# Decoder experts: where four final norms stand in VectorE's queue

## The chip, the cores and the metric

The kernel is one launch on one core of a Trainium2 chip. The metric is the device time of the launch in microseconds; a time is the median of several runs. Engines are called as in the profile: PE is TensorE (PEld its weight loads), DVE is VectorE, ACT is ScalarE, POOL is GpSimd, SP is SyncE, which here only issues DMAs.

## The reference

Two decoder layers work on 16 batches of 128 tokens by 512 features. Each layer has three blocks, each with a residual sum and a layer norm behind it:

```python
def _layernorm(x, axis=-1, eps=1e-05):
    m = jnp.mean(x, axis=axis, keepdims=True)
    v = jnp.var(x, axis=axis, keepdims=True)
    return (x - m) / jnp.sqrt(v + eps)
...
x = _layernorm(x + _L0_attn_ref(x, ...))    # state space scan
x = _layernorm(x + _L0_xattn_ref(x, ctx, ...))
x = _layernorm(x + _L0_ffn_ref(x, ...))
x = _layernorm(x + _L1_attn_ref(x, ...))
x = _layernorm(x + _L1_xattn_ref(x, ctx, ...))
x = _layernorm(x + _L1_ffn_ref(x, ...))     # 8 groups of experts
return x
```

The change touches only what follows the last block, so that block matters. It routes each token to 8 of 64 experts in 8 groups of 8 and sums over the groups that the token reaches:

```python
scores = softmax(x @ gate_w.T)
topk_w, topk_idx = top_k(scores, 8)
w_e = zeros((N, 64)).at[arange(N)[:, None], topk_idx].add(topk_w)
flat = w_e[:, inv_map]                      # N x 8 groups x 8
scalar = flat.sum(-1)
soft = softmax(where(flat == 0, NEG_INF, flat), axis=-1)
xg = x[:, None, :] + einsum('ngi,ghi->ngh', soft, mask_up_w)
a = silu(einsum('ngh,gih->ngi', xg, gate_proj_w)) * einsum('ngh,gih->ngi', xg, up_proj_w)
y = einsum('ng,ngh->nh', scalar, einsum('ngi,ghi->ngh', a, down_proj_w))
```

## The kernel before

Five stages follow one another: `stage_ssm`, `stage_xattn`, `stage_ffn`, `stage_attention`, `stage_moe`. The residual stream stays in SBUF as 16 tiles `k.x[b]`, one for each batch.

The expert stage, `stage_moe`, works on two halves of 8 batches. The router (`Moe.route`) has scattered a copy of each token's row into a bucket in DRAM for each group that the token reaches. Each half's buckets hold up to 768 rows, six tiles of 128. A *unit* is one such tile of one group: units 0 to 47 are the first half's 8 groups, units 48 to 89 seven groups of the second half, and the last group of the second half is done for all tokens of its 8 batches, in order, without a bucket (units 90 to 97).

One software-pipelined loop, `for t in range(-5, len(units) + 4)`, runs over the units. A step `t` does the following parts, each for another unit, named by their distance:

- `fetch` (unit t+5): SP loads the tile `row` from its bucket, six buffers.
- `places` (t+3) and `masks` (t+2): PE transposes part of the row (`pts`, L1507) and multiplies by the mask weights (`pm`, L1513); DVE adds the row: `xg` (L1515).
- `turn_in` (t+1): four PE transposes `ptx` of `xg` (L375, in `transpose4`), copied by ACT into `xgT` (L1521).
- `gate_up` (t): 16 PE matmuls into `pg` and `pu` (L1529), one PSUM buffer each; ACT takes `act` from `pg` (L1532), DVE multiplies it with `pu` (L1533).
- `turn_act` (t-1): PE transposes `pta` (L1539), ACT copies `aT` (L1541).
- `down` and `store` (t-2): six PE matmuls `y` (L1546); DVE copies `y` into `yo` (L1556), and ACT issues the store `results<-yo` (L1557).

The weights of a group, `gu` and `dn` (`Moe.load`), are loaded by SP into two buffers, one group ahead.

Once a unit's result is stored, `Moe.combine` runs as a generator, one `yield` a step. POOL gathers the group's results for one batch into `got` (L1565), three steps later POOL adds them to `k.x[b]` (L1572), and four steps later, in the last group of the first half and for every second batch, `self.finish(b - 1)` writes the final norm of two batches. So the norms of batches 0/1, 2/3, 4/5 and 6/7 are written as the generators of these pairs end. `finish` calls `layernorm` (statistics L68, aggregate L69, scaling L72) and with it `rsqrt` (three Newton steps of small operations, L53 to L58), all on DVE, and then issues two `out` transfers on SP (L1582). The norms of the second half are written by `store`, at the end of the kernel.

The order in which the program writes instructions is not the order in which an engine runs them. A scheduler orders each engine's instructions by when it takes their operands to be ready; each engine then works through its queue strictly in that order, waiting at each instruction for its semaphores. `tc.keep_in_program_order(ins)` binds an instruction behind what has been written before it for the same engine. Before the change only some PE transposes and matmuls elsewhere use it, by the class `Side`. In the compiled queue of before, the norms of the first half stand among the DVE instructions of steps 45 to 50. As the program writes them, they come at the ends of steps 53, 55 and 57 (two pairs in the last).

Of the kernel before, what the change touches and what calls it, by code (L numbers as in the profile page):

```python
# [13 lines left out]
I32 = mybir.dt.int32  # L14
U8 = mybir.dt.uint8
AF = mybir.ActivationFunctionType
ALU = mybir.AluOpType
# [25 lines left out]
        self.n += 1  # L43


def rsqrt(k, v, n, eps, scale=1.0):


    nc = k.nc
    a = k.small.tile([P, n], F32, tag=f"rs_a{n}", name="rs_a")  # L50
    y = k.small.tile([P, n], F32, tag=f"rs_y{n}", name="rs_y")
    t = k.small.tile([P, n], F32, tag=f"rs_t{n}", name="rs_t")
    nc.vector.tensor_scalar(a, v, scale, eps, ALU.mult, ALU.add)  # L53
    nc.vector.tensor_scalar(y.bitcast(I32), a.bitcast(I32), -0.5, 1597463007.0, ALU.mult, ALU.add)
    for _ in range(3):
        nc.vector.tensor_tensor(t, y, y, ALU.mult)
        nc.vector.scalar_tensor_tensor(t, t, -0.5, a, ALU.mult, ALU.mult)
        nc.vector.scalar_tensor_tensor(y, t, 1.5, y, ALU.add, ALU.mult)  # L58
    return y


def layernorm(k, ins, outs, eps=1e-5):

    nc, n = k.nc, len(ins)
    mv = k.small.tile([P, n, 2], F32, tag=f"ln_mv{n}", name="ln_mv")
    for i, r in enumerate(ins):
        st = k.small.tile([P, nc.vector.BN_STATS_DIM], F32, tag="ln_st", name="ln_st")
        nc.vector.bn_stats(st, r)  # L68
        nc.vector.bn_aggr(mv[:, i, :], st)  # L69
    rstd = rsqrt(k, mv[:, :, 1], n, eps)  # L70
    for i, (r, o) in enumerate(zip(ins, outs)):
        nc.vector.tensor_scalar(o, r, mv[:, i, 0:1], rstd[:, i : i + 1], ALU.subtract, ALU.mult)  # L72


def stage_ssm(k):
# [9 lines left out]
    with ExitStack() as ctx:  # L85
# [96 lines left out]
        def output(p, ys):  # L182

            mv = k.small.tile([P, BQ, 2], F32, tag="s1_mv", name="s1_mv")
            xs = k.x[p * BQ : (p + 1) * BQ]
            for i, x in enumerate(xs):
                po = bank("BA"[i], [P, D], "po")
                for c in range(KC):
                    nc.tensor.matmul(po, ys[c // 2][:, c % 2, i * P : (i + 1) * P], outw[:, c], start=c == 0, stop=False)
                nc.tensor.matmul(po, ones[32:33, 0:P], rows[32:33], start=False, stop=True)  # L190
                nc.vector.tensor_tensor(x, po, x, ALU.add)
                st = k.small.tile([P, nc.vector.BN_STATS_DIM], F32, tag="ln_st", name="ln_st")
                nc.vector.bn_stats(st, x)
                nc.vector.bn_aggr(mv[:, i, :], st)
                yield
            rstd = rsqrt(k, mv[:, :, 1], BQ, 1e-5)
            shift = k.small.tile([P, BQ], F32, tag="s1_sh", name="s1_sh")
            nc.vector.scalar_tensor_tensor(shift, mv[:, :, 0], -1.0, rstd, ALU.mult, ALU.mult)
            for i, x in enumerate(xs):
                nc.scalar.activation(x, x, AF.Identity, scale=rstd[:, i : i + 1], bias=shift[:, i : i + 1])  # L200
            yield
# [202 lines left out]
def stage_xattn(k):  # L404
# [9 lines left out]
    with ExitStack() as ctx:  # L414
# [54 lines left out]
        def project(b):  # L469
# [44 lines left out]
            yield  # L514
            nc.scalar.copy(st.v[:, 0], ps)
            rk = rsqrt(k, ss[:, 0:8], 8, EPS, 1.0 / HD)
            for s, kr in enumerate(krs):
                nc.gpsimd.tensor_tensor(kr, kr, rk[:, 4 * s : 4 * s + 4].unsqueeze(2).to_broadcast([P, 4, HD]), ALU.mult)
# [71 lines left out]
        def outputs(st, g):  # L590

            yield
            ao = pao.tile([P, J * P], F32, tag="ao", name="ao")
            for s in range(2):
                nc.tensor.matmul(
                    ao, st.v[:, s, g * HD : (g + 1) * HD], st.pTs[g][:, s].rearrange("p j t -> p (j t)"), start=s == 0, stop=s == 1
                )
            yield
            aT = wk.tile([P, J, P], F32, tag="aT", name="aT", bufs=3)
            nc.vector.tensor_copy(aT.rearrange("p h t -> p (h t)"), ao)  # L600
            yield
            if g == 0:
                st.po = pao.tile([P, D], F32, tag="po", name="po")
            for j in range(J):
                h = g * J + j
                nc.tensor.matmul(st.po, aT[:, j], k.wo[h // 8][:, h % 8], start=h == 0, stop=h == G * J - 1)  # L606
            yield
            if g == G - 1:
                nc.vector.tensor_tensor(k.x[st.b], st.po, k.x[st.b], ALU.add)
                yield  # L610
                if st.b % 2:
                    xs = k.x[st.b - 1 : st.b + 1]
                    layernorm(k, xs, xs)
                    yield
# [92 lines left out]
def stage_ffn(k):  # L707
# [4 lines left out]
    with ExitStack() as ctx:  # L712
# [8 lines left out]
        def prepare(st):  # L721

            xn = [wk.tile([P, D], F32, tag="xn", name="xn") for _ in st.xs]
            layernorm(k, st.xs, xn, 1e-8)
            yield
            qs, st.step = quantize(k, xn)
            yield
            st.qT = []
            for q in qs:
                st.qT.append(transpose_q(k, po_, q))  # L730
                yield

        def finish(st):
            layernorm(k, st.xs, st.xs)
            yield
# [9 lines left out]
        for n, sn in enumerate(states):  # L745
            nxt = prepare(states[n + 1]) if n + 1 < len(states) else iter(())
            for i, x in enumerate(sn.xs):
                st = sn.step[:, i : i + 1]
                po = po_.tile([P, D], F32, tag="po", name="po")
                for h in range(HB):  # L750
# [24 lines left out]
                    if n and h >= 2:  # L775
                        next(ahead, None)
                nc.vector.tensor_tensor(x, po, x, ALU.add)
            late = finish(sn)
        for _ in late:
            pass  # L780
# [517 lines left out]
class Moe:  # L1298
# [260 lines left out]
    def combine(self, h, g, n):  # L1559

        k, nc, b = self.k, self.nc, h * (NB // 2) + n
        got = self.wk.tile([P, D], F32, tag="got", name="got", bufs=10)

        end = 1 + min(P * (n + 1), self.CAP)
        nc.gpsimd.indirect_dma_start(  # L1565
            out=got[:, :], out_offset=None, in_=k.results[h][g][0:end, :],
            in_offset=bass.IndirectOffsetOnAxis(ap=self.gidx[:, b, g : g + 1], axis=0),
        )
        yield
        yield  # L1570
        yield
        nc.gpsimd.tensor_tensor(k.x[b], got, k.x[b], ALU.add)  # L1572
        for _ in range(4):
            yield
        if g == self.NG - 1 and n % 2:
            self.finish(b - 1)

    def finish(self, b):
        xs = self.k.x[b : b + 2]
        layernorm(self.k, xs, xs)  # L1580
        for i, x in enumerate(xs):
            self.nc.sync.dma_start(self.k.args["out"][b + i], x)  # L1582

# [209 lines left out]
```

## Time and profile before

| | |
|---|---|
| median of 3 runs | 3377.56 us (3376.58 to 3380.5) |
| profiled execution | 3382.4 us, of which the span is 3380.6 us |
| granted PE clock, mean over the span | 0.965 |
| busy PE / DVE / ACT / POOL | 3153.0 / 1876.7 / 1379.5 / 1389.5 us |
| L1529, `pg` and `pu`, 784 matmuls each | 301.7 and 299.6 us |
| L1546, `y`, 588 matmuls | 268.3 us |
| L1572, POOL's sums, 120 | 152.2 us, 1274 ns each |
| L68, norm statistics, 96 | 65.4 us, 687 ns each |
| L1582, `out` transfers, 16 | issued from 2924.5 to 3374.7 us |

Busy time is the sum of the instructions' durations on an engine; the engines work beside each other, so the sums do not add up to the span. In the rows of a timeline the first number is the start in us from the span's begin, the second the length of one or of several merged instructions, then engine, line, operation, output and inputs. A bracket at the end holds the idle time of that engine just before, and what ended it. The names leave out buffer numbers: `x` is any of the 16 tiles.

### The profile page before, as it was taken

How to read it: one execution, taken by the hardware profiler on the slowest of the kernel's cores; microseconds unless marked ns; L12 is line 12 of the kernel's file. 1: busy time of each engine (PE TensorE's matmuls, PEld its weight loads, DVE VectorE, ACT ScalarE, POOL GpSimd, SP SyncE). 2: the span in 40 equal slices, each digit the busy share in tenths (PEclk: the TensorE clock that was granted, in tenths of full speed). 3: DMA queues.
4: the chain of work that ended last, by engine and by line, in shares of the span. 5: the costliest groups of instructions: out<-in, count | busy, mean ns of one | idle time of the engine just before them, and what ended most of it. 6: DMA issues, size and time to landing. Idle time of an engine off the chain costs nothing. (4 is left out here: it accounts for less than half of the span.)

```text
span 3380.6 us, 38522 instructions
## 1 busy us (share of the span) xinstructions
PE 3153.0 (93%) x12894; PEld 1813.6 (54%) x12944; DVE 1876.7 (56%) x4202; ACT 1379.5 (41%) x3299; POOL 1389.5 (41%) x1198
## 2 busy tenths in 40 slices
PE   6888999899999999999799989998989999989998
PEld 3444444355555555555466555665655566556665
DVE  5877888456556556455576669765643232222223
ACT  4655655133333233234333379865643232112221
POOL 6967887133323333332000066325624454233331
PEclk8999999899999999999899989999999999999999
DMA  6887332200000000002200010013335665445441
GB/s 230 261 259 223 98 88 69 68 7 4 7 4 4 7 4 4 7 1 94 91 1 1 17 47 1 11 57 148 137 133 175 201 233 189 163 156 172 163 158 65
DMA packets 161553, 317.28 MB, mean 94 GB/s; under 512 B 19113, under 2 KB 82089, under 8 KB 158276
## 3 DMA queue, kind: packets, MB, share of 16 engines
q1 hardware_dynamic: 123012, 215.83, 20.8%
q0 software_dynamic: 19328, 64.56, 5.5%
q10 hardware_dynamic: 19008, 34.35, 2.7%
q8 instruction: 105, 1.72, 0.2%
q14 instruction: 100, 0.82, 0.1%
HBM read 238.80 MB, written 129.04 MB: 109 GB/s over the span
## 5 line engine op out<-in xcount | busy, mean ns | idle before, releaser
L245 POOL TENSOR_TENSOR dBx<-dtx,BC 128x1024 f32<-128x1024 f32 x128 | 301.2, 2373 | 44.8 <-DVE h L258 35.1
L1529 PE MATMUL pg<-gu,xgT 128*128 128x352 f32 x784 | 301.7, 467 | 0.0
L1529 PE MATMUL pu<-gu,xgT 128*128 128x352 f32 x784 | 299.6, 464 | 0.0
L1546 PE MATMUL y<-dn,aT 128*128 128x512 f32 x588 | 268.3, 592 | 0.0
L1533 DVE SCALAR_TENSOR_TENSOR act<-pu,row,act 128x352 f32<-128x352 f32 x98 | 57.1, 583 | 376.3 <-PE pu L1529 317.9
L575 POOL TENSOR_TENSOR pr<-pr,sm 128x512 f32<-128x512 f32 x128 | 134.7, 1053 | 289.6 <-DVE sm L574 244.2
L236 ACT ACTIVATE h<-dt,negA 128x254 f32<-128x254 f32 x512 | 239.8, 474 | 14.9 <-DVE dt L178 2.1
L1572 POOL TENSOR_TENSOR x<-got,x 128x512 f32<-128x512 f32 x120 | 152.2, 1274 | 226.4 <-DMA got<-results,gidx 225.2
L606 PE MATMUL po<-w,aT 128*128 128x512 f32 x512 | 232.2, 597 | 1.1 <-DVE aT L600 1.1
L483 PE MATMUL pq<-w,xT 128*128 128x512 f32 x512 | 228.9, 594 | 0.0
L1565 POOL DMA_INDIRECT got<-results,gidx x120 | 116.2, 968 | 268.9 <-DMA results<-yo 216.1
L460 POOL TENSOR_TENSOR m<-m,m 128x512 f32<-128x512 f32 x96 | 121.6, 1267 | 247.0 <-DVE m L455 247.0
L258 DVE TENSOR_TENSOR_SCAN h<-h,dBx 128x1024 f32<-128x1024 f32 x80 | 183.0, 2294 | 71.0 <-ACT h L236 48.7
L568 ACT ACTIVATE pr<-sc,mx,sf 128x256 f32<-128x256 f32 x256 | 142.8, 562 | 187.0 <-DVE mx L561 176.1
L267 PE MATMUL py<-hC,ident 128*128 128x512 f32 x320 | 164.6, 643 | 49.1 <-ACT y L272 49.1
L1529 PEld LDWEIGHTS pu<-gu,xgT 128*128 128x128 f32 x784 | 151.2, 193 | 85.1 <-issue 4.2
L1529 PEld LDWEIGHTS pg<-gu,xgT 128*128 128x128 f32 x784 | 144.1, 194 | 64.7 <-issue 3.0
L1532 ACT ACTIVATE act<-pg 128x352 f32<-128x352 f32 x98 | 45.5, 464 | 318.6 <-PE pg L1529 248.9
L1546 PEld LDWEIGHTS y<-dn,aT 128*128 128x128 f32 x588 | 104.1, 190 | 100.8 <-issue 94.2
L1521 ACT COPY xgT<-ptx 128x512 f32<-128x512 f32 x98 | 57.5, 587 | 233.9 <-PE ptx L375 209.6
L483 PEld LDWEIGHTS pq<-w,xT 128*128 128x128 f32 x512 | 93.5, 190 | 102.0 <-issue 99.0
L606 PEld LDWEIGHTS po<-w,aT 128*128 128x128 f32 x512 | 95.4, 191 | 96.9 <-issue 92.9
(363 smaller groups left out, 6808.3 us busy)
## 6 DMA issues: line engine op xcount, KB each, us to landing
bucket<-zeros SPq DMA_DIRECT2D x96, 388.0 KB
row<-bucket SPq DMA_DIRECT2D x90, 388.0 KB
BC<-bcd SPq DMA_DIRECT2D x128, 256.0 KB
results<-yo ACTq DMA_DIRECT2D x90, 256.0 KB
gu<-in_moe_guT SPq DMA_DIRECT2D x16, 1408.0 KB
cT<-in_ctxT SPq DMA_DIRECT2D x32, 256.0 KB
dn<-in_moe_downT SPq DMA_DIRECT2D x16, 512.0 KB
rows<-r_row SPq DMA_DIRECT2D x16, 388.0 KB
```

What stands on the lines that cost most here:

```text
L236: nc.scalar.activation(h[:, c, :, 1:], st.dt[:, c].rearrange("p (b t) -> p b t", b=BQ)[:, :, 1:], AF.Exp, scale=negA[:, c, n : n + 1])
L245: nc.gpsimd.tensor_tensor(dBx, st.dtx, BC[:, 0].unsqueeze(1).to_broadcast([P, KC, TQ]), ALU.mult)
L258: nc.vector.tensor_tensor_scan(hf, hf, df, 0.0, ALU.mult, ALU.add)
L267: nc.tensor.matmul(st.py[c], k.ident, st.hC[n][:, 2 * c : 2 * c + 2], start=n == 0, stop=n == NS - 1)
L460: nc.gpsimd.tensor_tensor(m1, m1, m2, ALU.add)
L483: nc.tensor.matmul(ps, src[:, c], w[c], start=c == 0, stop=c == KC - 1)
L568: nc.scalar.activation(pr[:, j], st.sc[g, i][:, j], AF.Exp, scale=st.sf[:, h : h + 1], bias=st.mx[g, i][:, j : j + 1], accum_out=sm[:, j : ...
L575: nc.gpsimd.tensor_tensor(pr, pr, sm.unsqueeze(2).to_broadcast([P, 2, 2 * P]), ALU.mult)
L606: nc.tensor.matmul(st.po, aT[:, j], k.wo[h // 8][:, h % 8], start=h == 0, stop=h == G * J - 1)
L1529: nc.tensor.matmul(ps, u.xT[:, c], gu[:, c, lo : lo + I], start=c == 0, stop=c == KC - 1)
L1546: self.nc.tensor.matmul(u.y, u.aT[:, c], u.w[1][:, c], start=c == 0, stop=c == 2)
L1572: nc.gpsimd.tensor_tensor(k.x[b], got, k.x[b], ALU.add)
```

## The change

`rsqrt` and `layernorm` take a function `keep` and apply it to each DVE instruction that they write. By default it does nothing. The first half's call of `finish` passes `tc.keep_in_program_order`, and it is written two steps later than before, so at the ends of steps 55, 57 and 59. The second half's norms pass no `keep`. What is computed stays the same.

```diff
-def rsqrt(k, v, n, eps, scale=1.0):
+def rsqrt(k, v, n, eps, scale=1.0, keep=lambda ins: ins):
...
-    nc.vector.tensor_scalar(a, v, scale, eps, ALU.mult, ALU.add)
+    keep(nc.vector.tensor_scalar(a, v, scale, eps, ALU.mult, ALU.add))
...
-        nc.vector.tensor_tensor(t, y, y, ALU.mult)
+        keep(nc.vector.tensor_tensor(t, y, y, ALU.mult))
...
-def layernorm(k, ins, outs, eps=1e-5):
+def layernorm(k, ins, outs, eps=1e-5, keep=lambda ins: ins):
...
-        nc.vector.bn_stats(st, r)
-        nc.vector.bn_aggr(mv[:, i, :], st)
-    rstd = rsqrt(k, mv[:, :, 1], n, eps)
+        keep(nc.vector.bn_stats(st, r))
+        keep(nc.vector.bn_aggr(mv[:, i, :], st))
+    rstd = rsqrt(k, mv[:, :, 1], n, eps, keep=keep)
...
-        nc.vector.tensor_scalar(o, r, mv[:, i, 0:1], rstd[:, i : i + 1], ALU.subtract, ALU.mult)
+        keep(nc.vector.tensor_scalar(o, r, mv[:, i, 0:1], rstd[:, i : i + 1], ALU.subtract, ALU.mult))
...
         if g == self.NG - 1 and n % 2:
-            self.finish(b - 1)
-
-    def finish(self, b):
+            for _ in range(2):
+                yield
+            self.finish(b - 1, self.k.tc.keep_in_program_order)
+
+    def finish(self, b, keep=lambda ins: ins):
         xs = self.k.x[b : b + 2]
-        layernorm(self.k, xs, xs)
+        layernorm(self.k, xs, xs, keep=keep)
         for i, x in enumerate(xs):
             self.nc.sync.dma_start(self.k.args["out"][b + i], x)
```

More of the change, by code (lines that the diff above doesn't have):

```diff
@@ L52, in rsqrt @@
     t = k.small.tile([P, n], F32, tag=f"rs_t{n}", name="rs_t")
-    nc.vector.tensor_scalar(a, v, scale, eps, ALU.mult, ALU.add)
-    nc.vector.tensor_scalar(y.bitcast(I32), a.bitcast(I32), -0.5, 1597463007.0, ALU.mult, ALU.add)
+    keep(nc.vector.tensor_scalar(a, v, scale, eps, ALU.mult, ALU.add))
+    keep(nc.vector.tensor_scalar(y.bitcast(I32), a.bitcast(I32), -0.5, 1597463007.0, ALU.mult, ALU.add))
     for _ in range(3):
-        nc.vector.tensor_tensor(t, y, y, ALU.mult)
-        nc.vector.scalar_tensor_tensor(t, t, -0.5, a, ALU.mult, ALU.mult)
-        nc.vector.scalar_tensor_tensor(y, t, 1.5, y, ALU.add, ALU.mult)
+        keep(nc.vector.tensor_tensor(t, y, y, ALU.mult))
+        keep(nc.vector.scalar_tensor_tensor(t, t, -0.5, a, ALU.mult, ALU.mult))
+        keep(nc.vector.scalar_tensor_tensor(y, t, 1.5, y, ALU.add, ALU.mult))
     return y
-def layernorm(k, ins, outs, eps=1e-5):
+def layernorm(k, ins, outs, eps=1e-5, keep=lambda ins: ins):
     nc, n = k.nc, len(ins)
@@ L1575, in combine @@
         if g == self.NG - 1 and n % 2:
-            self.finish(b - 1)
-    def finish(self, b):
+            for _ in range(2):
+                yield
+            self.finish(b - 1, k.tc.keep_in_program_order)
+    def finish(self, b, keep=lambda ins: ins):
         xs = self.k.x[b : b + 2]
-        layernorm(self.k, xs, xs)
+        layernorm(self.k, xs, xs, keep=keep)
         for i, x in enumerate(xs):
```

## The prediction

> **What bounds the kernel now.** I read the page's busy shares first: PE is busy 3153.0 of 3380.6 us (93%), so a gain must come from PE's few idle places. Then I followed the chain of work that ended last. In the expert stage it is PE at one constant beat, except between 2889 and 2976 us, where it leaves PE and goes round by DVE, two DMAs and POOL. The waits of 2880 to 2990 us name the two links:
>
> ```profile
> DVE ln_st L68 <- POOL x L1572: 38.1, 7, 8.4
> PE ptx L375 <- DVE xg L1515: 14.4, 5, 7.3
> ```
>
> Columns: us in total, times, the longest. DVE stood 38.1 us in front of seven statistics of a final norm (L68) whose batch POOL had not yet summed; PE stood 14.4 us in front of five transposes (L375) that need `xg`, queued on DVE behind them. The windows cut this at PE's `y` matmuls: six steps before the disturbance, the five disturbed steps together, six steps after, then the two worst alone (length, then busy time of PE, PEld, DVE, ACT and POOL, granted clock, DMA share, GB/s):
>
> ```profile
> 2872.21:2922.74 50.53, 50.53 (x188) 30.75 (x187) 12.94 (x29) 9.48 (x23) 16.84 (x15) 1.00 0.48 155
> 2922.74:2983.68 60.94, 46.54 (x157) 27.33 (x156) 23.56 (x75) 8.66 (x22) 16.75 (x15) 0.92 0.49 163
> 2983.68:3034.20 50.52, 50.52 (x188) 30.74 (x187) 11.34 (x20) 10.19 (x25) 17.86 (x16) 1.00 0.52 165
> ...
> 2932.06:2945.76 13.70, 10.30 (x33) 6.01 (x32) 4.59 (x15) 1.59 (x4) 3.50 (x3) 0.88 0.27 86
> ...
> 2965.80:2983.52 17.72, 10.40 (x34) 6.19 (x32) 9.68 (x37) 2.14 (x6) 6.65 (x6) 0.81 0.40 134
> ```
>
> A normal step is 50.53 / 6 = 8.42 us with PE full. The middle row holds five steps, so it is 60.94 - 5 x 8.42 = 18.84 us too long. PE's timeline shows the idle part at each transpose:
>
> ```profile
> 2926.19 0.63 PE L375 MATMUL ptx<-ident,xg 128*128 128x128 f32 x4 [0.87 <-DVE xg L1515]
> 2938.20 0.78 PE L375 MATMUL ptx<-ident,xg 128*128 128x128 f32 x4 [3.40 <-DVE xg L1515]
> 2949.38 0.63 PE L375 MATMUL ptx<-ident,xg 128*128 128x128 f32 x4 [0.87 <-DVE xg L1515]
> 2959.93 0.63 PE L375 MATMUL ptx<-ident,xg 128*128 128x128 f32 x4 [1.94 <-DVE xg L1515]
> 2975.86 1.09 PE L375 MATMUL ptx<-ident,xg 128*128 128x128 f32 x4 [7.32 <-DVE xg L1515]
> ```
>
> That is 14.40 us idle. The other 4.4 us are matmuls run slower right after a stall: 13.70 - 8.42 - 3.40 = 1.9 us and 17.72 - 8.42 - 7.32 = 2.0 us in the two steps whose clock is 0.88 and 0.81, 0.2 us in each of the others.
>
> **The change, part by part.** I number a step by the unit whose gate and up matmuls it holds. In DVE's compiled queue of before, the four norms of batches 0 to 7 lie in steps 45 to 50, each first statistic in front of `yo`. In the changed queue they lie behind `yo` of steps 55, 57 and 59, the fourth running over into step 60. Nothing is added: DVE still does 8 statistics, 8 aggregates, 44 small operations and 8 scalings. No instruction on PE, ACT or POOL changes place; on SP only the eight `out` transfers move.
>
> *Removed:* the seven waits on POOL. They made `yo` late, with it ACT's store, ACT's `act` queued behind that store, DVE's `act` and `xg`, and so PE's transpose. Gain: 18.84 us, all of it, since both neighbours of the stretch run with PE full at clock 1.00, and every chain piece after 2976 us up to the last units is PE. What is late next in those steps is PE itself.
>
> *The waits at the new place.* POOL's last sums for batches 0 to 7 end at 2911 to 2969 us. Step 55's `yo` starts at 3011.56 us, less 18.84 = 2992.7 us; the last pair's norm comes four steps later, at about 3032 us. Each sum is at least 57 us early. Cost 0, cover 57 us.
>
> *The DVE time at the new place.* The stretch that it must fit into, from DVE's and PE's timelines (start, length, idle before in brackets):
>
> ```profile
> 2986.30 0.69 DVE L1556 COPY yo<-y 128x512 f32<-128x512 f32 x1 [1.99 <-PE y L1546]
> 2991.53 0.58 DVE L1533 SCALAR_TENSOR_TENSOR act<-pu,row,act 128x352 f32<-128x352 f32 x1 [4.54 <-PE pu L1529]
> 2992.03 0.69 DVE L1515 TENSOR_TENSOR xg<-pm,row 128x512 f32<-128x512 f32 x1
> 2994.52 0.60 PE L375 MATMUL ptx<-ident,xg 128*128 128x128 f32 x4
> ```
>
> A norm with no wait in it is the last one of the kernel:
>
> ```profile
> 3370.57 0.69 DVE L68 BATCH_NORM_STATS2 ln_st<-x 128x6 f32<-128x512 f32 x1
> 3371.29 0.18 DVE L69 BATCH_NORM_AGGREGATE ln_mv<-ln_st 128x2 f32<-128x6 f32 x1
> 3371.51 0.17 DVE L53 TENSOR_SCALAR rs_a<-ln_mv 128x2 f32<-128x2 f32 x1
> 3373.68 1.00 DVE L72 TENSOR_SCALAR x<-x,ln_mv,rs_y 128x512 f32<-128x512 f32 x2
> ```
>
> Statistics to aggregate 0.72, aggregate to the second statistics 0.10, again 0.72, aggregate to the inverse root 0.22, its eleven operations 2.17, both scalings 0.9: 4.83 us. `yo` lets the next instruction start after 0.60 us, so `act` comes 0.60 + 4.83 - (2991.53 - 2986.30) = 0.20 us late. `xg` ends at 2992.72 and in the disturbed steps a transpose follows its end by 0.15 us (2938.05 to 2938.20), so `xg` may be 2994.52 - 2992.72 - 0.15 = 1.65 us late for nothing. Steps 55 and 57 cost PE 0. In step 60 a whole norm and one statistic (0.60) lie in front of `act`, and an aggregate and a statistic (0.7) between `act` and `xg`: `xg` is 0.20 + 0.60 + 0.70 = 1.5 us late, just inside 1.65. Cost 0, but this cover is nearly used up. `yo` of step 60 is about 0.9 us late; nothing on ACT's queue behind its store is due for 3 us.
>
> *POOL beside the norms.* In before the norms mostly began when POOL had just finished; now they start on a schedule and can meet POOL at work. One pair of rows shows a meeting:
>
> ```profile
> 2965.26 3.72 POOL L1572 TENSOR_TENSOR x<-got,x 128x512 f32<-128x512 f32 x3 [1.80 <-DMA got<-results,gidx]
> ...
> 2968.40 0.60 DVE L53 TENSOR_SCALAR rs_a<-ln_mv 128x2 f32<-128x2 f32 x1
> ```
>
> The small operation normally takes 0.17 us; here it ended (2969.00) with POOL's third sum (2968.98), while a statistic at 2967.79 ran its usual 0.69 us beside the same sum. The Trainium skill, "SBUF — State Buffer", section "Who interferes with whom", speaks against the change here: VectorE's second port pair is shared with GpSimd under an exclusive lock, and an instruction with two SBUF inputs or in a two-port mode is blocked for GpSimd's whole instruction. Nearly every small operation of the norm qualifies. By that rule at its worst, all POOL time of a step, 17.86 / 6 = 3.0 us, is added to a norm: against 1.65 - 0.20 = 1.45 us of cover 1.5 us in each of steps 55 and 57, against 0.15 us 2.8 us in step 60, together 5.8 us. By the rows, POOL in before does this in the stretches of the same steps:
>
> ```profile
> 3029.70 1.27 POOL L1572 TENSOR_TENSOR x<-got,x 128x512 f32<-128x512 f32 x1 [3.02 <-DMA got<-results,gidx]
> ```
>
> It meets the norm of step 57 (3029.0 to 3033.8 on that clock), mostly its statistics, and holds the first small operation by some 0.2 us; nothing of POOL falls on steps 55 or 59; in step 60 a gather (3051.43) meets a statistic, and a sum (3055.47) the tail behind `yo`. I take 0 and keep 5.8 us as the bad end. A gain from here is excluded: PE has no idle time left there.
>
> *SP's queue.* The eight transfers move from between the row fetches of units 52 to 57 to behind the weights of group 10 (`dn`, step 55), between the fetches of units 61 to 67, in pairs, each just after its norm. In before, the first pair held `gu` of group 9 to 2925.43 us where the beat of 50.53 us (2871.57 before) puts it at 2922.10. In after, a row fetch is free only when `act` of six units earlier is done, and that is queued behind the same norm, so an `out` in front of it adds its issue, about 0.4 us a transfer. A row is first read three steps (25 us) later, and `gu` of group 11, issued in step 59, in step 66. Cost 0.
>
> Sum: 18.84 gained, 0 paid. The profiled execution took 3382.4 us with a span of 3380.6; its like after the change is 3361.8 us of span, 3363.6 in all. That execution stands 4.84 us above the median of the timed runs, 3377.56. From the median: 3377.56 - 18.84 = 3358.7 us, 0.56% less.
>
> **The rivals.** *A part only (7 to 14 us gained).* The stall depends on how late gathers land, and the timed runs could hold less of it: were the whole 4.84 us between profile and median missing stall, the gain there would be 14.0 us, 3363.6 us. A half-paid gain also comes if the port lock strikes at its worst: 3358.7 + 5.8 = 3364.5. Against both: the beat is the same to 0.01 us on both sides of the stretch, and POOL's timeline leaves the new places nearly free. With some new wait of rows or weights in steps 45 to 50 I would expect about 3368 us; against it, no such wait shows in the six steps before or after.
>
> *Nothing moves (within 0.2%).* The stall is covered by another of the same size at the same place. Against: DMA share is 0.5 there, as in its full-speed neighbours; it would need 12 us or more of new stall.
>
> *Slower.* The pinned norm still finds POOL behind, and now nothing can be put in front of it: `act`, `xg`, ACT's store and SP's row fetches wait with it. It decides once POOL's sums come more than 57 us (their lead) and 1.45 us (DVE's cover) later than in this trace. To be slower by over 6.8 us the four norms must cost 18.84 + 6.8 = 25.6 us, 6.4 us each and so a lag of about 65 us: 3358.7 + 25.6 = 3384.3 us. POOL is busy 18 of every 50 us and drains each group within the next, so I give this little.
>
> **How the numbers follow.** 0.2% is 6.8 us, about what a measurement of this kernel can tell from no change. Full gain 0.87; a part 0.07; nothing 0.03; slower 0.03. So faster 0.94, same 0.03, slower 0.03. Range: down to 3354.8 (the runs of before spread over 3.9 us, so one such spread below the forecast), up to 3364.7, which takes in both ends of the partial case (3363.6 and 3364.5).
>
> **What would show it.** Right: no wait of DVE's L68 on POOL behind step 44; every `y` to `y` distance 8.42 us through steps 45 to 66; clock 1.00; the `out` issues behind `dn` of group 10; span near 3361.8. Wrong: a transpose L375 idle on `xg` in steps 56 to 61 (the norms don't fit), rs operations of over 0.5 us (port), a PE wait on `row` or `gu` (SP), or L68 waiting on POOL at the new place.

## The result, and the profile after

The changed kernel took 3364.69 us (median of 6 runs, 3356.05 to 3368.03), the kernel before on the same chip 3377.31 us (6 runs, 3376.58 to 3382.89): a ratio of 0.9951 with a 95% interval of 0.9941 to 0.9961. It is faster, by 12.6 us, where the forecast had 18.84; the time lies 0.01 us inside the upper end of the stated range, 3364.7. The profiled execution took 3364.07 us with a span of 3362.3 us, where the forecast had 3363.6 and 3361.8.

In the stretch that the change touches, the trace agrees with the forecast. (That the whole spans agree to 0.5 us is partly luck: these are single executions, and the work ahead of the expert loop alone differs by up to 9 us between the traces below.) The chain of work that ended last, by engine, from the page of after:

```profile
PE 21%; DVE 0%; issue 0%; DMA 0%; POOL 0%; ACT 0%; POOLq 0%; DVEq 0%; ACTq 0%
```

Before it was PE 19%, DMA 2%, DVE and POOL 1% each; the detour over gathers, sums and statistics is gone from it. Three stretches of six steps each from where the stall began, as windows of after (length, busy time of PE, PEld, DVE, ACT and POOL, granted clock, DMA share, GB/s):

```profile
2922.58:2973.11 50.53, 50.53 (x188) 30.74 (x187) 11.34 (x18) 10.20 (x24) 18.09 (x17) 1.00 0.49 164
2973.11:3023.63 50.52, 50.52 (x188) 30.75 (x187) 20.60 (x52) 10.20 (x24) 17.87 (x16) 1.00 0.57 187
3023.63:3074.17 50.54, 50.54 (x188) 30.76 (x187) 20.42 (x52) 10.20 (x24) 17.76 (x16) 1.00 0.56 185
```

PE is full and its clock 1.00 throughout. DVE's work has moved: 11.34 us in the first row, where before it did the norms, and 20.60 and 20.42 in the next two, where it does them now. Over 2880 to 3100 us the waits of after have no row of L68 on POOL and none of a PE transpose on `xg`; the first rows are the ordinary ones of the beat:

```profile
DVE act L1533 <- PE pu L1529: 105.5, 24, 4.6
ACT act L1532 <- PE pg L1529: 82.2, 24, 3.5
```

The tightest place is the fourth norm, from DVE's timeline of after:

```profile
3023.74 0.58 DVE L1533 SCALAR_TENSOR_TENSOR act<-pu,row,act 128x352 f32<-128x352 f32 x1 [4.56 <-PE pu L1529]
3024.24 0.68 DVE L1515 TENSOR_TENSOR xg<-pm,row 128x512 f32<-128x512 f32 x1
...
3032.94 0.57 DVE L1533 SCALAR_TENSOR_TENSOR act<-pu,row,act 128x352 f32<-128x352 f32 x1
3033.43 0.17 DVE L69 BATCH_NORM_AGGREGATE ln_mv<-ln_st 128x2 f32<-128x6 f32 x1
3033.51 0.66 DVE L68 BATCH_NORM_STATS2 ln_st<-x 128x6 f32<-128x512 f32 x1
3034.09 0.68 DVE L1515 TENSOR_TENSOR xg<-pm,row 128x512 f32<-128x512 f32 x1
```

The upper `xg` belongs to step 59, the lower to step 60. One beat later than 3024.24 would be 3032.66; it starts at 3034.09, 1.43 us late (1.5 forecast, 1.65 allowed), and PE's transpose comes on time at 3035.13. SP issues the `out` pairs at 2998.32, 3015.97, 3031.99 and 3039.07 us, and no PE instruction waits for a row or a weight.

### The profile page after: what moved, and what is told of

Its sections match the earlier page's. It is cut to its first block, busy times and chain, and to the rows that moved or that the text cites. A ratio compares the mean times of both kernels' runs of the same rounds, so it can differ in the third digit from the quotient of the medians.

```text
span 3362.3 us, 38572 instructions
## 1 busy us (share of the span) xinstructions
PE 3155.7 (94%) x12944; PEld 1814.9 (54%) x12944; DVE 1877.8 (56%) x4202; ACT 1380.7 (41%) x3299; POOL 1390.6 (41%) x1198
## 5 line engine op out<-in xcount | busy, mean ns | idle before, releaser
L1556 DVE COPY yo<-y 128x512 f32<-128x512 f32 x90 | 62.2, 692 | 158.0 <-PE y L1546 142.4
```

## The experiments

My theory: the seven waits are all that the change takes away, they cost their full 18 to 19 us in every run, and the norms cost nothing where they stand now. The rivals: timed runs hold a shorter stall than the trace of before; or the norms cost PE some 6 us at the new place, through the port that DVE shares with POOL. Either would explain 12.6 us instead of 18.84.

To compare the traces I took the starts of PE's `y` matmuls, one for each step, and subtracted 8.42 us a step. "Too long" below means that.

**The two halves of the change.** `e1_pin_only` keeps the norms in order but leaves out the two steps; `e2_late_only` has the two steps but leaves the order to the scheduler.

```diff
# e1_pin_only, against the change
-            for _ in range(2):
-                yield
             self.finish(b - 1, k.tc.keep_in_program_order)
# e2_late_only, against the change
-            self.finish(b - 1, k.tc.keep_in_program_order)
+            self.finish(b - 1)
```

> One part alone: the norms are kept in their written place, but written at the old steps, so they stand behind yo of steps 53, 55 and 57 instead of 55, 57 and 59. Theory (the place behind finished sums is what counts, and two steps more or less do not): POOL's sums are still over 40 us early, no wait of L68 on POOL, the same time as the change within 0.1%, so about 3364 us by the timed runs. Rival (the two steps are needed because the sums come late in some runs): L68 waits on POOL again and part of the 12 us is lost, 3367 us or more.

> The other part alone: written two steps later, but not kept there, so the scheduler places the norms itself. DVE's and SP's compiled queues come out as in the kernel before, so the run is also a second trace of the old order. Theory: nothing is gained, 3377 us within 0.2%, and the stretch of steps 47 to 51 is again 18 to 19 us longer than five steps of 8.42 us; the 6 us that the timed runs lack against the forecast then lie in the spread of the other stages. Rival (the trace of before was an execution with a long stall, and most have less): the stretch is only 12 to 15 us too long.

`e1_pin_only` took 3365.07 us (ratio to before 0.9946, 0.9933 to 0.9959), `e2_late_only` 3383.24 us (1.0003, 0.9995 to 1.0011); the runs of before beside them had a median of 3383.18 us (19 runs). So keeping the order is nearly the whole change; two steps later without it is nothing, since the scheduler puts the norms back where they were. `e2_late_only` is thereby a second trace of the old order. Its waits over 2880 to 2990 us:

```profile
DVE ln_st L68 <- POOL x L1572: 37.1, 7, 8.2
...
PE ptx L375 <- DVE xg L1515: 13.9, 5, 7.3
```

Again seven waits and five stalls, and five steps that are 17.9 us too long (60.02 against 42.1).

The two steps have a small use that I did not foresee. In `e1_pin_only` one step is 8.88 us, 0.46 too long:

```profile
3008.32 1.27 POOL L1572 TENSOR_TENSOR x<-got,x 128x512 f32<-128x512 f32 x1 [3.24 <-DMA got<-results,gidx]
...
3008.80 0.82 DVE L53 TENSOR_SCALAR rs_a<-ln_mv 128x2 f32<-128x2 f32 x1
...
3015.12 0.63 PE L375 MATMUL ptx<-ident,xg 128*128 128x128 f32 x4 [0.27 <-DVE ln_mv L69]
```

The place with two norms lies two steps earlier there and meets a POOL sum: the first small operation lasts 0.82 us instead of 0.17, until the sum ends, and the cover of 1.65 us is overdrawn. The profile names the aggregate L69 as releaser, which stands beside `xg` in the queue.

**The ceiling.** `e3_no_norm` leaves out the first half's four norms and stores the sums.

```diff
-        layernorm(self.k, xs, xs, keep=keep)
+        if b >= NB // 2:
+            layernorm(self.k, xs, xs, keep=keep)
```

> The first half's four norms are left out, the sums are stored as they are; the second half's norms stay. This is the ceiling of any placing of these norms. Theory (at the new place they cost PE nothing): the same time as the change within 0.1%, about 3364 us. Rival (in the timed runs the norms meet POOL on the shared port and cost what is lacking): about 6 us faster than the change, 3358 us.

3363.87 us, ratio 0.9946 (0.9933 to 0.9959), the same as the change run beside it (`e4_after_again`, below). Each of the two intervals is some 4 us wide to either side, so these medians alone would not exclude a small cost. The traces do: in both traces of the change every step in which DVE works on the norms is at the beat. The norms cost PE nothing where they stand, and the rival with the shared port falls as an explanation of the missing 6 us.

**The change again.**

> The change itself, once more, beside the other three on one chip and with a second trace. Theory: 11 to 15 us faster than the kernel before by the timed runs; the trace has every y to y distance of steps 45 to 66 at 8.42 us. Rival (the regular steps were one lucky execution): one or more steps above 9 us near steps 55 to 61.

3364.03 us, ratio 0.9948 (0.9935 to 0.9961): the median lies 19.15 us below the 3383.18 of before, more than the 11 to 15 that I had written, since before was slower when run beside it. All steps from 45 to 66 are at the beat.

**Where the cover ends.** `e6_four_at_once` writes all four norms at the end of step 59.

```diff
-            for _ in range(2):
+            for _ in range(8 - min(n, 5) + 1 - 2):
                 yield
```

> All four norms written at the end of step 59, still kept in order, so that DVE has 19.3 us of norms from there on; its queue then has act, xg and yo of steps 60 and 61 in between. It tests the cover that the forecast worked out (xg may come 1.65 us late). By that arithmetic xg of step 60 is 1.5 us late as in the change, for nothing; in front of act of step 61 lie the rest of the second norm's root and most of the third norm, 2.1 us more than the gap, and two scalings and a statistic between act and xg, so xg is about 3.6 us late and PE loses about 2 us, once, at the transpose of step 62: 3362 us of span become about 3364. Rival (DVE has more room than that, xg of one step is not what PE's next transpose waits for): every step 8.42 us. Rival (the shared port adds POOL's time to the norms): 4 us or more lost.

3371.51 us, ratio 0.9967 (0.9955 to 0.9979). In the trace one step is too long, the one between `y` of steps 61 and 62, by 13.74 - 8.42 = 5.3 us, not 2:

```profile
3042.50 1.27 POOL L1572 TENSOR_TENSOR x<-got,x 128x512 f32<-128x512 f32 x1 [3.65 <-DMA got<-results,gidx]
3047.99 1.26 POOL L1572 TENSOR_TENSOR x<-got,x 128x512 f32<-128x512 f32 x1 [3.10 <-DMA got<-results,gidx]
...
3042.41 2.10 DVE L72 TENSOR_SCALAR x<-x,ln_mv,rs_y 128x512 f32<-128x512 f32 x2
3048.14 1.14 DVE L58 SCALAR_TENSOR_TENSOR rs_y<-rs_t,rs_y 128x2 f32<-128x2 f32 x1
...
3052.02 0.63 PE L375 MATMUL ptx<-ident,xg 128*128 128x128 f32 x4 [3.44 <-DVE ln_mv L69]
```

PE stands for 3.44 us of it. The two scalings take 2.10 us instead of 1.00 and a small operation 1.14 instead of 0.16, each held by a sum of POOL: 2.1 us of the 3.44. That leaves 1.3 us for DVE's own work, where the arithmetic of the cover had 2; it named the right step. The rest, 1.9 us, is slower matmuls after the stall. Both the theory and the port rival are needed for this kernel. The median lies 7.8 us above that of `e7_earliest` (below), which ran beside it; that is 2.5 us more than the trace explains, and three of the ten runs took only 3362 to 3367 us. Whether the stall comes in every run is not shown.

**The earliest place.** `e7_earliest` writes each norm right behind its last sum.

```diff
-        for _ in range(4):
-            yield
         if g == self.NG - 1 and n % 2:
-            for _ in range(2):
-                yield
             self.finish(b - 1, k.tc.keep_in_program_order)
+            return
+        for _ in range(4):
+            yield
```

> Kept in order, and written right behind the last sum instead of six steps later, the earliest place that the program can write: behind yo of steps 49, 51 and 53. In the trace of the change the sums of the three places are done about 25, 22 and 9 us before that. Theory (a norm costs PE nothing as soon as its sum is done before DVE reaches it): the same time as the change within 0.1%, no wait of L68 on POOL. Rival (the added steps are needed): L68 waits for POOL in step 53 or 54, and PE loses 2 us or more.

3363.75 us, ratio 0.9946 (0.9928 to 0.9964), no wait of L68, every step from 45 to 66 at the beat. The order is what counts, as long as the sum is done first. (In the change's trace the last of the third place's sums is done at 2957.17 us, 19 us before `yo` of step 53, not 9.)

**The stall again, and the spread.**

> The kernel before, once more, for a third trace of its stall. Theory (the stall is always there, 18 to 19 us, and the spread of the timed runs comes from other stages): the five steps from 47 to 51 are 17.5 to 19.5 us longer than 42.1 us whatever the time of the run. Rival (the first timed runs of before, at 3377 us, held a shorter stall): a stall below 16 us, in a run that is below 3379 us.

3385.22 us (ratio 1.0008, 0.9997 to 1.0019), five steps 18.6 us too long. The run was not a short one, so it does not try the rival's case.

**The same sign elsewhere.** The change's trace has two more places where PE stands, steps 10 and 18. The waits of after over 2570 to 2605 us show the cause of the first:

```profile
DVE act L1533 <- ACT act L1532: 21.0, 2, 11.4
ACT r_row L1459 <- DMA bucket<-r_row,r_to: 16.6, 2, 9.3
...
PE ptx L375 <- DVE xg L1515: 4.1, 1, 4.1
```

This time ACT is the one that waits at the head of its queue. It copies a batch into a row tile (L1459) that earlier scatters are still reading, and its `act`, DVE's `act` and `xg` and PE's transpose wait behind. In step 18 it stands there for another 16.0 us, in two waits. `e5_more_rows` gives the tiles eight buffers.

```diff
-        rows = [wr.tile([P, self.ROW], F32, tag="r_row", name="r_row", bufs=4) for _ in range(2)]
+        rows = [wr.tile([P, self.ROW], F32, tag="r_row", name="r_row", bufs=8) for _ in range(2)]
```

> The change, and the router's row tiles (r_row) in eight buffers instead of four. In the trace of the change two places of the expert stage are left with PE idle, steps 10 and 18 (15.6 and 18.7 us from y to y, where such steps otherwise take 8.9 and 10.2): ACT stands up to 11 us at the head of its queue in the copy into r_row (L1459), until the scatters of the rows before have read the buffer, with ACT's act and so DVE's act, xg and PE's transpose behind it. Theory (the same sign as the stall that the change took away: a finished neighbour queued behind a wait for data): with buffers of their own the copies wait for nothing, both steps fall to about 9 and 10 us, and the kernel gains about 15 us on the change, to about 3349 us. Rival (POOL, which issues the scatters one after the other at 1.3 us each, sets the pace, and the wait moves to the next tile that it uses): the same time as the change within 5 us.

3349.86 us, ratio to before 0.9910 (0.9895 to 0.9924). The two steps, as windows of after and then of `e5_more_rows`:

```profile
2585.70:2601.30 15.60, 11.48 (x38) 7.03 (x37) 1.78 (x3) 2.59 (x6) 12.81 (x13) 0.78 0.60 222
2663.90:2682.60 18.70, 13.33 (x50) 8.73 (x49) 4.05 (x15) 5.56 (x10) 9.00 (x9) 0.73 0.41 146
```

```profile
2585.30:2594.20 8.90, 8.90 (x38) 5.60 (x37) 1.94 (x4) 2.33 (x6) 7.31 (x8) 1.00 0.74 260
2656.80:2667.00 10.20, 10.20 (x50) 6.95 (x49) 3.80 (x15) 4.62 (x8) 6.18 (x6) 1.00 0.70 262
```

6.7 and 8.5 us are gone, 15.2 in all, and the wait of L1459 on the scatters with them. By the timed runs it is 13.9 us faster than `e7_earliest`, a form of the change that ran beside it. The copies did not only lose their wait, they also moved: in after the last four start at 2590.7, 2602.1, 2655.4 and 2671.4 us, with eight buffers at 2477.1 to 2491.6 us, ahead of the first `y`. So the run shows what these copies cost where they waited, but not what free buffers alone would give at the old place.

**The change alone, with the row tiles out of the way.** `e9_before_rows` is the kernel before with the eight buffers, `e10_rows_again` is `e5_more_rows` once more beside it.

> The kernel before with r_row in eight buffers, so without the two uneven stalls of steps 10 and 18, which differ by 2 us each from trace to trace; only the norms' waits are left in the expert stage. Beside it on the same chip runs the same with the change (e10_rows_again), so the pair measures the change alone with less spread. Theory (the change is worth its whole stall in every run, 17.9 to 18.8 us in three traces of the old order): 18 us above e10_rows_again, about 3368 us, and five steps 18 to 19 us too long. Rival (only part of the stall is paid in timed runs, as the first 12.6 us of measured gain would say): 12 to 14 us above it.

> The change with r_row in eight buffers, once more, as the partner of e9_before_rows. Theory: about 3350 us again, no step of the expert stage above 10.2 us. Rival (the 15 us of the first measurement were a draw of its chip): 3355 us or more.

3369.25 us (ratio 0.9959, 0.9945 to 0.9972) and 3346.44 us (0.9896, 0.9881 to 0.9912): 22.8 us apart, with a stall of 19.7 us in the first one's trace and none in the second's. The rival had 12 to 14 us. In the traces the excess over the stall lies ahead of it: the first one's is also 5.6 us later at the first `y`.

## Why the prediction was right, point by point

*The waits.* Right in place, cause and size. Four traces of the old order hold 18.8, 17.9, 18.6 and 19.7 us of it; all eight traces with the norms kept one after another behind their sums or left out hold none in steps 47 to 51. The waits also fed themselves. The forecast named the chain round by DVE, two DMAs and POOL, but drew nothing from it: `yo` behind a waiting norm made its store late, the store POOL's gather, and the gather the sum that the next norm waits for. The last sum of the first half ended at 2968.98 us in before and at 2957.17 us in after, in the same order of POOL's work, so part of the lateness that the norms met was their own doing.

*The norm's length and the cover.* From `yo` to the next `act` the first norm took 2998.66 - 2993.23 = 5.43 us, as summed (0.60 + 4.83); `xg` of step 60 was 1.43 us late against 1.5. The limit of 1.65 us fits, to 0.2 us, the two kernels that crossed it: in `e1_pin_only` `xg` was 2.07 us late and PE stood 0.27, in `e6_four_at_once` 5.27 late and PE stood 3.44.

*POOL's port.* I took 0 for PE, which held. One of the signs of being wrong that the forecast named did show, an `rs` operation of over 0.5 us; it cost PE nothing. The size was off: I expected a hold of some 0.2 us in step 57, and it was 0.8, since POOL's sum sits elsewhere once the stall is gone (3012.10 us, where the old timeline less 18.84 us had 3010.86):

```profile
3012.10 1.27 POOL L1572 TENSOR_TENSOR x<-got,x 128x512 f32<-128x512 f32 x1 [3.00 <-DMA got<-results,gidx]
...
3012.41 0.99 DVE L53 TENSOR_SCALAR rs_a<-ln_mv 128x2 f32<-128x2 f32 x1
```

`xg` was about 1.0 us late there, still inside the cover. The Trainium skill's rule ("SBUF — State Buffer", "Who interferes with whom") speaks of a full block, and the rows agree: the held operation ends with POOL's sum, at 3013.4 us. Overlaying POOL's old timeline on the new order was the weak step; it gave the right answer with less room than it said.

*SP.* Right: the weights of group 9 went out at 2922.60 us (forecast 2922.10, in a trace whose stage ran 0.5 us later), and the row fetches behind an `out` pair went out 0.0 to 1.0 us behind the beat, for which PE never waited.

*The level.* This is the term that was mis-sized. "3377.56 - 18.84" took a median of three runs as the level of before. The first six runs of it lie low: four of them are below 3377.6 us, and only four of the 49 runs of before beside the experiments are. These 49, in three groups, have medians of 3383.2, 3383.5 and 3383.9 us, and against those the change's 3364 to 3365 us is 19 us, the forecast's gain. The two profiled executions are 3382.4 - 3364.07 = 18.3 us apart.

By its number alone the first comparison looks like the forecast's partial rival, with 7 to 14 us gained. No trace supports that rival, but none refutes it for those runs: no execution of before as short as 3377 us was traced. Why they were short stays open. So there is luck in the range having held. Its upper end came from a shorter stall and from POOL's port, and neither was seen to cost anything in the change's traces.

A spread of some microseconds comes from ahead of the change. Over the twelve traces the first `y` starts anywhere between 2510.0 and 2519.2 us, and with four row buffers the next 28 steps take 263.8 to 269.3 us (with eight, 250.4 to 250.6 in three traces), while the last 30 steps take 251.4 us in each.

## What to carry to other kernels

In these traces DVE (38.1 us in seven waits) and ACT (32.6 us in four) stood in front of one instruction whose data were late, with work of finished operands queued behind it. So an instruction that a scheduler places ahead of its operands does harm through its neighbours: look for an engine that waits on slow data while the bound engine waits for what is queued behind it, and move the waiting instruction behind its data, or give it a buffer of its own. Before moving it, work out the gap that it must fit into and the lateness that the next consumer allows, and leave room for an engine that shares a port. Take the gain from the stretch itself in several traces: here the median of the first three runs lay 6 us below that of the later ones, a third of the gain.

## What the runs showed of the hardware

- A small DVE operation of the norms (0.16 to 0.17 us) that met a POOL sum of 1.27 us lasted 0.60 to 1.27 us, thirteen times in eleven traces, and each time ended within 0.03 us of the sum's end. Scalings were held too (1.96 and 2.10 us for two instead of 1.00), the first of the two ending 0.28 us after the sum. Statistics (0.69 us) and aggregates (0.18 us) ran at their usual length beside a sum.
- Ten stalls of PE of 2.5 to 7.3 us in steps 47 to 61 (five traces) cost the step a further 1.6 to 3.0 us of slower matmuls, and eleven of 0.27 to 2.02 us cost a further 0.2 each. Behind each of the ten the granted clock was 0.50 for 3.41 or 6.83 us (in before from 2938.54 and from 2972.68 us), and 1.00 behind each of the eleven. No stall between 2.02 and 2.50 us was seen there.
- The beat of 8.42 us held to 0.01 us in twelve traces, in every step from 30 to 93 outside the stretches with these stalls.
